# The second attention's normalisation moved by a step each, its transpose into another PSUM bank, and its value pads written in one copy

## The chip, the cores and the metric

The kernel runs on one core of one Trainium2 chip. The metric is the device time of one execution in microseconds (us). A core has five engines with a queue each: TensorE (PE in the profile; its weight loads are PEld), VectorE (DVE), ScalarE (ACT), GpSimd (POOL) and SyncE (SP), which only issues DMAs here. PSUM, where TensorE's results land, has eight banks, and GpSimd does not work on it in this kernel.

## The reference

Two layers of a gated cross-attention block over x of 16 x 128 x 256 (batches, tokens, channels), with a context of the same shape:

```python
x = x + tanh(g_xattn[0]) * L0_xattn(layernorm(x), ctx, ...)   # first attention, fp8-rounded inputs, 16 heads of 128
x = x + tanh(g_ffn[0])   * L0_ffn(layernorm(x), ...)          # silu feed-forward
x = x + tanh(g_xattn[1]) * L1_xattn(layernorm(x), ctx, ctx, mask, ...)
x = x + tanh(g_ffn[1])   * L1_ffn(layernorm(x), ...)          # top-1 mixture of 8 experts
```

The change lies in the third line, the second attention. Its core, for each of the 16 batches:

```python
q = (Q @ w_q.T).reshape(B, S, 8, 4, 8)        # 32 heads of 8: 8 groups of 4
k = (K @ w_k.T).reshape(B, S, 8, 8)           # one key and one value head for each group
v = (V @ w_v.T).reshape(B, S, 8, 8)
scores = einsum("bnghd,bmgd->bnghm", q, k) / sqrt(8)
scores = where(pad or not causal, -inf, scores)
attn = softmax(scores, axis=-1)
out = einsum("bnghm,bmgd->bnghd", attn, v).reshape(B, S, 256)
return out @ w_o.T + b_o
```

## The kernel before

The program is unrolled. Its stages follow one another with some overlap: first attention (lines 239 to 665), feed-forward (694 to 732), second attention (858 to 1156) with the routing of the tokens to experts (785 to 856) woven in, and the experts (1169 to 1213).

**The second attention** is a loop over steps n (line 1123). A step is 8 of a batch's 32 heads, 128 queries by 128 keys each, so a batch is four steps and a pair of steps is one half (c) of the output's 256 channels. At step n the loop writes down, in this order:

- scores(n) and top(n): TensorE adds the mask (L992, an identity matmul in bf16) and the scores (L999) in a PSUM tile of two banks, of which there are two; VectorE takes the negated maximum of each row (L1006). The keys come as kb, each group's keys masked to one head's rows.
- probs(n - 1): TensorE transposes the exponentials e of the step before (L1034, eight 128x128 blocks into two banks tagged tr), and VectorE copies them to eT (L1035, two copies).
- exp(n): ScalarE writes e, unnormalised (L1015, eight instructions), and GpSimd halves the rows three times by addition, to 16 partial sums for each row (L1021, L1022, L1023: half, half, part).
- values(n - 2), for odd n: VectorE sums the 16 partial sums of the pair's 16 heads (L1045) and takes the reciprocal (L1046); GpSimd spreads it over the 8 channels of a head (L1048: rr, one buffer); TensorE multiplies eT with the value pads (L1052, 16 matmuls, each to 32 output rows) into o, the first half of the PSUM bank tagged pv.
- divide(n - 3), for even n: TensorE transposes rr into the second half of the same bank (L1067), ScalarE copies that to rsum in SBUF (L1069), and VectorE multiplies o with rsum into oT (L1070).
- keys of the batch two steps ahead: GpSimd makes kb (L970, two instructions), TensorE the values (L976, PSUM tag mm), and VectorE copies them four times (L981) into the value pad. A pad holds, for each group and each of its four heads, 32 columns of which only the head's own 8 aren't zero, so that the four heads' matmuls add up to 32 output rows. There are two pads, zeroed once.
- for every fourth batch's start, the front of the next group of four: load, norm, transposes (L940), query and key projections (L952, tag mm).
- the routing's stages, then output of batch (n - 4) // 4 when its last step's division is done: TensorE projects oT (L1076, tag mm), VectorE adds the bias (L1078) and the residual (L1082) into a row. When a routing group (4, 4, 4, 3 and 1 batches) is complete, routing starts: norm, transposes, the router's matmuls (L798, tag mm), its decision on VectorE, prefix counts by matmul (L827, L828, tag mm), and then for each batch a store of the plain row (SP, L856) and a scatter of the row to its expert's slot (GpSimd's queue, L845). The experts' loads wait for all scatters.

PSUM's eight banks in this stage: four for the scores, two tr, one pv, one mm. So all users of mm follow one another, each waiting until the one before has been read out.

**What sets the order.** Semaphores and buffers are handled by a tile framework. It also orders each engine's instructions: a planner runs through the program with its own forecast of times and gives a free engine the ready instruction that ranks first, by the written order (the score matmuls rank 100 places earlier). So an engine's order can differ from the written one, and once set it is fixed: on the chip an engine waits at the head of its queue.

```python
    for n in range(-2, N1 + 5):
        ...
        if 0 <= n - 2 < N1:
            values(n - 2)
        if 0 <= n - 3 < N1:
            divide(n - 3)
```

Of the kernel before, what the change touches and what calls it, by code (L numbers as in the profile page):

```python
# [9 lines left out]
F32 = mybir.dt.float32  # L10
# [5 lines left out]
ALU = mybir.AluOpType  # L16
AX = mybir.AxisListType

P = 128
B = 16  # L20
DM = 256
KD = DM // P
# [13 lines left out]
def flamingo_kernel(  # L36
# [27 lines left out]
    nc = tc.nc  # L64
# [4 lines left out]
    NH, NG, HD = 32, 8, 8  # L69
# [4 lines left out]
    psum = psum0.enter_context(tc.tile_pool(name="psum", bufs=2, space=bass.MemoryType.PSUM))  # L74
# [36 lines left out]
    ident = const.tile([P, P], F32, name="ident")  # L111
# [127 lines left out]
    with (  # L239
# [74 lines left out]
        class Unit:  # L314
# [162 lines left out]
            def scores(self, c):  # L477
                qT = self.qT.pop(c)
                pscore = ps_sc([P, 4, P])
                for j in range(4):  # L480
                    nc.tensor.matmul(  # L481
                        pscore[:, j, :], qT[:, j, :], self.kT[:, 2 * c + j // 2, :],
                        start=True, stop=True,
                    )
                self.sc[c] = pscore

            def top(self, c):
                mx = small.tile([P, 4], F32, tag="mx", name="mx")
                nc.vector.tensor_reduce(mx, self.sc[c], AX.X, ALU.max, negate=True)  # L489
                self.mx = mx  # L490
# [12 lines left out]
            def recip(self, c):  # L503
                sums = self.e[c][1]
                nc.vector.reciprocal(sums, sums)  # L505

            def divide(self, c):
                e, sums = self.e[c]
                nc.gpsimd.tensor_tensor(  # L509
                    e, e, sums[:, :, None].to_broadcast([P, 4, P]), ALU.mult  # L510
                )
# [10 lines left out]
            def values(self, c):  # L522
                eT = self.eT.pop(c)
                pv = ps_pv([P, 4, P])
                for g in range(2):
                    gg = 2 * c + g
                    nc.tensor.matmul(  # L527
                        pv[:, 2 * g : 2 * g + 2, :], self.vt[:, gg * P : (gg + 1) * P],
                        eT[:, 2 * g : 2 * g + 2, :], start=True, stop=True,
                    )  # L530
                self.pv[c] = pv
# [212 lines left out]
    NQ = NH // NG  # L744
# [151 lines left out]
    vpads = [cq.tile([P, NG, NQ, 32], F32, name=f"vpad{i}") for i in range(2)]  # L896
# [61 lines left out]
        else:  # L958
            nc.scalar.copy(f[i][:, c, :], pm)

    kbs, vps, es, eTs, oTs, scs, mxs, sums, pvs = {}, {}, {}, {}, {}, {}, {}, {}, {}

    def keys(b):

        g, j = divmod(b, G)
        f = front[g]
        tok = slice(j * P, (j + 1) * P)
        kb = ap.tile([P, KD, NQ, P], F32, tag="kb", name="kb")
        for c in range(KD):
            nc.gpsimd.tensor_tensor(  # L970
                kb[:, c], f[1][:, c, None, tok].to_broadcast([P, NQ, P]),
                hmask[:, :, None].to_broadcast([P, NQ, P]), ALU.mult,
            )
        pm = psum.tile([P, NG, HD], F32, tag="mm", name="ps_mm")
        for k in range(KD):
            nc.tensor.matmul(  # L976
                pm, f["cT"][:, k, tok], av[:, k, :], start=(k == 0), stop=(k == KD - 1)
            )
        vp = vpads[b % 2]
        for i in range(NQ):  # L980
            nc.vector.tensor_copy(vp[:, :, i, HD * i : HD * i + HD], pm)  # L981
        kbs[b], vps[b] = kb, vp

    def scores(n):
# [53 lines left out]
    def values(n):  # L1038

        if n % 2 == 0:  # L1040
            return
        b, c = n // 4, n // 2 % 2
        r = small.tile([P, 16], F32, tag="sum16", name="sum16")
        part = sums.pop(n // 2)
        nc.vector.tensor_reduce(r, part.rearrange("p i h t -> p (i h) t"), AX.X, ALU.add)  # L1045
        nc.vector.reciprocal(r, r)  # L1046
        rr = ap.tile([P, 16, HD], F32, tag="rr16", name="rr16", bufs=1)
        nc.gpsimd.tensor_copy(rr, r[:, :, None].to_broadcast([P, 16, HD]))  # L1048
        o = psum.tile([P, 2, P], F32, tag="pv", name="ps_pv", bufs=1)
        for h in range(NQ):  # L1050
            for q in range(4):
                nc.tensor.matmul(  # L1052
                    o[32 * q : 32 * q + 32, 0, :], vps[b][:, 4 * c + q, h, :],
                    eTs[n - 1 + q // 2][:, q % 2, h, :],
                    start=(h == 0), stop=(h == NQ - 1),
                )
        pvs[n] = o, rr

    def divide(n):

        if n % 2 == 0:
            return
        b, c = n // 4, n // 2 % 2
        o, rr = pvs.pop(n)
        if c == 0:
            oTs[b] = ap.tile([P, KD, P], F32, tag="oT", name="oT")
        nc.tensor.transpose(o[:, 1, :], rr.rearrange("p h d -> p (h d)"), ident)  # L1067
        rT = ap.tile([P, P], F32, tag="rsum", name="rsum", bufs=1)
        nc.scalar.copy(rT, o[:, 1, :])  # L1069
        nc.vector.tensor_tensor(oTs[b][:, c, :], o[:, 0, :], rT, ALU.mult)  # L1070

    def output(b):
        oT = oTs.pop(b)
# [26 lines left out]
    for g in range(B // G):  # L1100
# [3 lines left out]
        for b in range(g * G, (g + 1) * G):  # L1104
# [8 lines left out]
    ap = f2.enter_context(tc.tile_pool(name="a1", bufs=2, side="right", reuse_waits="tile"))  # L1113
    psum = f2.enter_context(
        tc.tile_pool(
            name="psum1", bufs=1, space=bass.MemoryType.PSUM, reuse_waits="tile"
        )
    )


    N1 = 4 * B
    routes = []
    for n in range(-2, N1 + 5):
        if 0 <= n < N1:
            scores(n)
            top(n)
        if 0 <= n - 1 < N1:
            probs(n - 1)
        if 0 <= n < N1:
            exp(n)  # L1130
        if 0 <= n < G:
            down(B - G + n, hd, psum.tile([P, DM], F32, tag="mm", name="ps_mm"))
            if n == G - 1:
                tp.close()
                ep = ctx.enter_context(tc.tile_pool(name="e1", bufs=2, reuse_waits="tile"))
        if 0 <= n - 2 < N1:
            values(n - 2)
        if 0 <= n - 3 < N1:
            divide(n - 3)
        m = n + 2  # L1140
        if m % 4 == 0 and 0 <= m < N1:
            keys(m // 4)
        g, i = divmod(n + 12, 16)
        if 1 <= g < B // G:
            front_step(g, i)
        for stages in routes:
            next(stages, None)
        m = n - 4
        if m % 4 == 3 and 0 <= m < N1:
            output(m // 4)  # L1150
            for b0, count in ROUTES:
                if m // 4 == b0 + count - 1:
                    routes.append(route(b0, count))
    for stages in routes:
        for _ in stages:
# [4 lines left out]
    psum = ctx.enter_context(  # L1160
        tc.tile_pool(
            name="psum2", bufs=2, space=bass.MemoryType.PSUM, reuse_waits="tile"
        )
    )
# [4 lines left out]
    for e in range(NE):  # L1169
# [12 lines left out]
        for f in range(NFC):  # L1182
            ph = ps_mm([P, CAP])
            for k in range(KD):
                nc.tensor.matmul(
                    ph, w1t[:, k, f * P : (f + 1) * P], xT[:, k, :],
                    start=(k == 0), stop=(k == KD - 1),
# [3 lines left out]
        for c in range(NCC):  # L1191
            po = ps_sc([P, DM])
            for f in range(NFC):
                nc.tensor.matmul(
                    po, hT[:, f, c * P : (c + 1) * P], w2t[:, f, :],
                    start=(f == 0), stop=(f == NFC - 1),
# [8 lines left out]
                    ap=xe[:, c, 2 * DM + 1 : 2 * DM + 2].bitcast(I32), axis=0  # L1205
# [79 lines left out]
```

## Time and profile before

| | |
|---|---|
| median of 3 runs | 1578.25 us (1572.7 to 1580.31) |
| the profiled execution | 1577.98 us, span from first to last instruction 1576.2 us |
| mean granted TensorE clock over the span | 0.950 |
| busy over the span: PE, DVE, ACT, POOL | 88%, 67%, 52%, 53% |
| first attention, from its first projection to its last residual | 27.0 to 953.6 us |
| second attention, from its first score to its last division or output | 1083.7 to 1432.8 us |
| experts | 1441.2 to 1572.4 us |
| L1045, sum, 128x16 out of 128x256, on VectorE | 32 times, 413 ns |
| L1046, reciprocal, on VectorE | 32 times, 247 ns |
| L1048, rr, on GpSimd | 32 times, 300 ns |
| L1067, transpose of rr | 32 times, 307 ns |
| L1069, rsum, on ScalarE | 32 times, 281 ns |
| L1070, division, on VectorE | 32 times, 280 ns |
| L981, value pad, 128x64, on VectorE | 64 times, 213 ns |
| L1078, bias, 128x256 out of PSUM, on VectorE | 16 times, 411 ns |

The columns of a group in the profile are: line, engine, operation, output and inputs, shapes and count, busy time, mean duration of one, idle time of the engine in front of it and what ended that. "A <- B: us, times, longest" in a list of waits says that A's engine stood idle until B released it. In a list in order of time the first two numbers are start and duration (us from the span's start), merged over instructions that follow one another; the brackets give the idle time in front and who ended it. Matmuls of fp32 operands show as two records each. The granted clock is 1 or 0.5 at any time; a mean between them is a mixture.

### The profile page before, as it was taken

The numbers are of one execution on the slowest core, as the hardware profiler recorded it, in microseconds if no ns is written. First come the engines' busy times: TensorE is split into PE (matmuls) and PEld (weight loads), VectorE is DVE, ScalarE is ACT, GpSimd is POOL, SyncE is SP. The second block draws the span as 40 slices with busy tenths as digits, with TensorE's granted clock in tenths as the row PEclk, the third lists the DMA queues.
The fourth block names the chain that finished last, engine by engine and source line by source line (L and its number), as shares of the span: only waits on it lengthen the run. The fifth ranks groups of instructions, "written<-read, shape, count | busy, mean of one in ns | idle before, by whom it ended". The sixth has DMA issues, their size and how long they took to land. (4 is left out here: it accounts for less than half of the span.)

```text
span 1576.2 us, 23047 instructions
## 1 busy us (share of the span) xinstructions
PE 1390.5 (88%) x7620; PEld 1002.1 (64%) x7620; DVE 1050.9 (67%) x2821; ACT 819.5 (52%) x2452; POOL 835.7 (53%) x793
## 2 busy tenths in 40 slices
PE   2878798798988999999999978999898899885998
PEld 1567677676765777777777764555445455554887
DVE  8888878788798776767676753534667677773100
ACT  3666566566566666666666641534444455441121
POOL 4566666667677555565656552121766766661111
PEclk9999999999999999999999988999998979885999
DMA  4301001000022100000000007000300100001562
GB/s 122 107 6 31 14 11 35 11 18 14 11 80 65 48 25 11 21 11 21 11 17 14 8 24 210 8 0 1 114 24 8 48 4 35 8 35 61 176 195 78
DMA packets 51113, 68.59 MB, mean 44 GB/s; under 512 B 5292, under 2 KB 37740, under 8 KB 50993
## 3 DMA queue, kind: packets, MB, share of 16 engines
q1 hardware_dynamic: 36912, 41.31, 8.6%
q10 hardware_dynamic: 11456, 17.63, 3.4%
q0 software_dynamic: 2624, 8.16, 1.4%
q8 instruction: 61, 1.00, 0.3%
q14 instruction: 60, 0.48, 0.1%
HBM read 50.53 MB, written 16.81 MB: 43 GB/s over the span
## 5 line engine op out<-in xcount | busy, mean ns | idle before, releaser
L509 POOL TENSOR_TENSOR e<-e,sums 128x512 f32<-128x512 f32 x128 | 139.9, 1093 | 234.2 <-DVE sums L505 128.9
L497 ACT ACTIVATE e<-ps_sc,mx 128x128 f32<-128x128 f32 x512 | 181.4, 368 | 92.7 <-DVE mx L489 83.8
L454 POOL TENSOR_TENSOR raw<-raw,q_r 128x512 f32<-128x512 f32 x192 | 208.6, 1116 | 34.5 <-DVE q_r L180 33.3
L431 DVE BATCH_NORM_STATS2 q_st<-raw 128x6 f32<-128x128 f32 x768 | 173.9, 278 | 67.0 <-ACT raw L422 66.6
L1015 ACT ACTIVATE e<-ps_sc,mx 128x128 f32<-128x128 f32 x512 | 139.8, 385 | 90.0 <-DVE mx L1006 85.9
L565 PE MATMUL ps_acc<-wp,cat 128*128 128x512 f32 x512 | 161.4, 439 | 17.7 <-POOL cat L227 15.5
L227 POOL TENSOR_TENSOR cat<-e_t,e_e 128x1024 fp32r<-128x1024 bf16 x64 | 136.3, 2129 | 53.8 <-DVE e_t L221 52.2
L463 PE MATMUL ps_tr<-ident,raw 128*128 128x128 f32 x768 | 121.3, 286 | 46.7 <-POOL raw L454 44.3
L481 PE MATMUL ps_sc<-kT,qT 128*128 128x128 f32 x1024 | 141.0, 281 | 16.6 <-ACT qT L472 16.5
L481 PEld LDWEIGHTS ps_sc<-kT,qT 128*128 128x128 f32 x1024 | 131.9, 194 | 34.3 <-ACT qT L472 28.5
L463 PEld LDWEIGHTS ps_tr<-ident,raw 128*128 128x128 f32 x768 | 94.8, 146 | 84.5 <-POOL raw L454 59.3
L519 ACT COPY eT<-ps_tr 128x512 f32<-128x512 f32 x128 | 75.4, 589 | 139.4 <-PE ps_tr L517 139.2
L1021 POOL TENSOR_TENSOR half<-e 128x512 f32<-128x512 f32 x64 | 81.2, 1269 | 120.5 <-ACT e L1015 116.8
L527 PE MATMUL ps_pv<-eT,vt 128*128 128x256 f32 x512 | 133.4, 382 | 1.0 <-DVE cat_y L538 1.0
L565 PEld LDWEIGHTS ps_acc<-wp,cat 128*128 128x128 f32 x512 | 96.6, 195 | 57.7 <-POOL cat L227 22.5
L422 ACT COPY raw<-ps_mm 128x512 f32<-128x512 f32 x192 | 113.7, 593 | 28.4 <-PE ps_mm L410 26.1
L527 PEld LDWEIGHTS ps_pv<-eT,vt 128*128 128x128 f32 x512 | 97.1, 192 | 30.8 <-issue 8.6
L538 DVE TENSOR_TENSOR cat_y<-ps_pv,r_sm 128x512 bf16<-128x512 f32 x128 | 86.9, 679 | 39.6 <-PE ps_pv L527 39.4
L472 ACT ACTIVATE qT<-ps_tr,hv 128x512 f32<-128x512 f32 x128 | 101.0, 789 | 23.0 <-PE ps_tr L463 21.1
L489 DVE TENSOR_REDUCE mx<-ps_sc 128x4 f32<-128x512 f32 x128 | 87.2, 681 | 27.5 <-PE ps_sc L481 27.5
L497 ACT ACTIVATION_READ_ACCUMULATOR e<-ps_sc,mx 128x1 f32 x512 | 105.2, 205 | 0.0
L1034 PEld LDWEIGHTS ps_tr<-ident,e 128*128 128x128 f32 x512 | 62.1, 150 | 61.7 <-ACT e L1015 35.0
(232 smaller groups left out, 2944.4 us busy)
## 6 DMA issues: line engine op xcount, KB each, us to landing
w1t<-in_w ACTq DMA_DIRECT2D x8, 1024.0 KB, 5.1
w2t<-in_w ACTq DMA_DIRECT2D x8, 1024.0 KB, 5.6
disp<-empty SPq DMA_DIRECT2D x16, 257.0 KB, 8.3
xe<-disp SPq DMA_DIRECT2D x8, 514.0 KB, 3.7
stage<-in_wprojT SPq DMA_DIRECT2D x16, 256.0 KB, 2.8
xg<-in_x SPq DMA_DIRECT2D x4, 512.0 KB, 3.9
xb<-in_x SPq DMA_DIRECT2D x16, 128.0 KB, 2.0
ctx<-in_ctxT SPq DMA_DIRECT2D x16, 128.0 KB, 2.2
```

The costliest lines, as they stand in the source:

```text
L227: nc.gpsimd.tensor_tensor(dst, t[:, part], e[:, part], ALU.subtract)
L422: nc.scalar.copy(raw.rearrange("p h d -> p (h d)"), pm)
L431: nc.vector.bn_stats(self.st[:, 4 * blk + j, :], self.raws[blk][:, j, :])
L454: nc.gpsimd.tensor_tensor(src, src, self.r[:, 4 * blk : 4 * blk + 4, None].to_broadcast([P, 4, P]), ALU.mult,)
L463: nc.tensor.transpose(pt[:, j, :], src[:, j, :], ident)
L472: nc.scalar.activation(dst, pt, AF.Identity, scale=hv[:, col : col + 1], bias=hv[:, col + 1 : col + 2])
L481: nc.tensor.matmul(pscore[:, j, :], qT[:, j, :], self.kT[:, 2 * c + j // 2, :], start=True, stop=True,)
L497: nc.scalar.activation(e[:, j, :], pscore[:, j, :], AF.Exp, bias=self.mx[:, j : j + 1], accum_out=sums[:, j : j + 1],)
L509: nc.gpsimd.tensor_tensor(e, e, sums[:, :, None].to_broadcast([P, 4, P]), ALU.mult)
L527: nc.tensor.matmul(pv[:, 2 * g : 2 * g + 2, :], self.vt[:, gg * P : (gg + 1) * P], eT[:, 2 * g : 2 * g + 2, :], start=True, stop=True,)
L565: nc.tensor.matmul(self.acc, self.cat[c // 2][:, h % 8, :], wpr[self.cross, c][:, j, :, :], start=(h == 0), stop=(h == 15),)
L1015: nc.scalar.activation(e[:, i, :], s[:, i // NQ, i % NQ, :], AF.Exp, bias=mx[:, i : i + 1])
```

## The change

In values, the sum, the reciprocal and rr are taken out and become recip, which the loop writes at n - 3; rr has the pool's two buffers. values now has o to itself in the bank pv and copies it to oT at once, on VectorE. divide moves from n - 3 to n - 4, so to odd n; it transposes rr into a tile of the bank mm and multiplies oT in place by it, straight from PSUM, so ScalarE's copy and rsum are gone. output moves one step on, to n - 5, and the loop is one step longer. In keys, the four copies into the value pad become one, which reads each value four times and writes with a step of 40 elements from head to head (32 columns and 8).

```diff
-        vp = vpads[b % 2]
-        for i in range(NQ):
-            nc.vector.tensor_copy(vp[:, :, i, HD * i : HD * i + HD], pm)
+        vp = vpads[b % 2][:]
+        to = bass.AP(vp.tensor, vp.offset, [vp.ap[0], [P, NG], [32 + HD, NQ], [1, HD]])
+        nc.vector.tensor_copy(to, pm[:, :, None, :].to_broadcast([P, NG, NQ, HD]))
...
         b, c = n // 4, n // 2 % 2
+        o = psum.tile([P, P], F32, tag="pv", name="ps_pv", bufs=1)
+        for h in range(NQ):
+            for q in range(4):
+                nc.tensor.matmul(
+                    o[32 * q : 32 * q + 32, :], vps[b][:, 4 * c + q, h, :],
+                    eTs[n - 1 + q // 2][:, q % 2, h, :],
+                    start=(h == 0), stop=(h == NQ - 1),
+                )
+        if c == 0:
+            oTs[b] = ap.tile([P, KD, P], F32, tag="oT", name="oT")
+        nc.vector.tensor_copy(oTs[b][:, c, :], o)
+
+    def recip(n):
+
+        if n % 2 == 0:
+            return
         r = small.tile([P, 16], F32, tag="sum16", name="sum16")
         part = sums.pop(n // 2)
         nc.vector.tensor_reduce(r, part.rearrange("p i h t -> p (i h) t"), AX.X, ALU.add)
         nc.vector.reciprocal(r, r)
-        rr = ap.tile([P, 16, HD], F32, tag="rr16", name="rr16", bufs=1)
+        rr = ap.tile([P, 16, HD], F32, tag="rr16", name="rr16")
         nc.gpsimd.tensor_copy(rr, r[:, :, None].to_broadcast([P, 16, HD]))
-        o = psum.tile([P, 2, P], F32, tag="pv", name="ps_pv", bufs=1)
...
-        pvs[n] = o, rr
+        rrs[n] = rr
...
-        o, rr = pvs.pop(n)
-        if c == 0:
-            oTs[b] = ap.tile([P, KD, P], F32, tag="oT", name="oT")
-        nc.tensor.transpose(o[:, 1, :], rr.rearrange("p h d -> p (h d)"), ident)
-        rT = ap.tile([P, P], F32, tag="rsum", name="rsum", bufs=1)
-        nc.scalar.copy(rT, o[:, 1, :])
-        nc.vector.tensor_tensor(oTs[b][:, c, :], o[:, 0, :], rT, ALU.mult)
+        rT = psum.tile([P, P], F32, tag="mm", name="ps_mm")
+        nc.tensor.transpose(rT, rrs.pop(n).rearrange("p h d -> p (h d)"), ident)
+        nc.vector.tensor_tensor(oTs[b][:, c, :], oTs[b][:, c, :], rT, ALU.mult)
...
-    for n in range(-2, N1 + 5):
+    for n in range(-2, N1 + 6):
...
         if 0 <= n - 3 < N1:
-            divide(n - 3)
+            recip(n - 3)
+        if 0 <= n - 4 < N1:
+            divide(n - 4)
...
-        m = n - 4
+        m = n - 5
         if m % 4 == 3 and 0 <= m < N1:
             output(m // 4)
```

More of the change, by code (lines that the diff above doesn't have):

```diff
@@ L959, in qk @@
             nc.scalar.copy(f[i][:, c, :], pm)
-    kbs, vps, es, eTs, oTs, scs, mxs, sums, pvs = {}, {}, {}, {}, {}, {}, {}, {}, {}
+    kbs, vps, es, eTs, oTs, scs, mxs, sums, rrs = {}, {}, {}, {}, {}, {}, {}, {}, {}
     def keys(b):
@@ L1046, in values @@
         nc.vector.reciprocal(r, r)
-        rr = ap.tile([P, 16, HD], F32, tag="rr16", name="rr16", bufs=1)
+        rr = ap.tile([P, 16, HD], F32, tag="rr16", name="rr16")
         nc.gpsimd.tensor_copy(rr, r[:, :, None].to_broadcast([P, 16, HD]))
-        o = psum.tile([P, 2, P], F32, tag="pv", name="ps_pv", bufs=1)
[L1050 to L1056, printed above, removed]
-        pvs[n] = o, rr
+        rrs[n] = rr
     def divide(n):
```

## The prediction

> **What bounds the kernel now.** I read the page first, then the stretch of the second attention, its waits, and its instructions in order of time. The chain that ended last reaches back only to 1556.58 us, so it says nothing here. Slices 28 to 36 of the page (39.4 us each) are this stage:
>
> ```profile
> span 1576.2 us, 23047 instructions
> ...
> PE   2878798798988999999999978999898899885998
> ...
> PEclk9999999999999999999999988999998979885999
> ```
>
> TensorE is nine tenths busy in most of these slices, and the granted clock falls. The same stretch in one row:
>
> ```profile
> core 0: us, PE busy (x) PEld busy (x) DVE busy (x) ACT busy (x) POOL busy (x), PEclk, DMA share, GB/s
> 1085.00:1424.00 339.00, 300.02 (x2274) 174.14 (x2270) 242.55 (x548) 161.56 (x582) 218.78 (x274) 0.89 0.10 33
> ```
>
> TensorE is busy 300 of 339 us at a mean clock of 0.89. The clock record has only 1 and 0.5, so some 22% of the stretch, 75 us, ran at half clock; the work done there, 75 x 0.88 = 66 us, would take 33 us at full clock. No engine is full. Who waits, from 1110 to 1420 (total, times, longest, in us):
>
> ```profile
> ACT e L1015 <- DVE mx L1006: 75.4, 45, 6.0
> ...
> DVE sum L1045 <- POOL part L1023: 35.7, 13, 4.1
> ...
> PEld ps_tr L1034 <- ACT e L1015: 35.0, 28, 2.8
> ...
> PE ps_tr L1034 <- ACT e L1015: 12.8, 9, 2.0
> PE ps_pv L1067 <- POOL rr L1048: 12.2, 7, 3.5
> ...
> PE ps_pv L1052 <- DVE oT L1070: 4.2, 1, 4.2
> ```
>
> Three waits stop TensorE itself: 12.8 us for e, 12.2 us for rr, 4.2 us for oT. Behind the first is VectorE, which stood 35.7 us in its sum waiting for GpSimd's partial sums. The order of time shows how:
>
> ```profile
> 1165.13 1.13 PE L999 MATMUL ps_sc<-kb,qT 32*128 32x512 f32 x4
> ...
> 1168.74 0.29 POOL L1048 COPY rr<-sum 128x128 f32<-128x128 f32 x1
> ...
> 1169.09 0.33 PE L1067 MATMUL ps_pv<-ident,rr 128*128 128x128 f32 x1 [1.81 <-POOL rr L1048]
> ...
> 1169.80 0.45 POOL L1023 TENSOR_TENSOR part<-half 128x128 f32<-128x128 f32 x1
> 1170.28 0.42 DVE L1045 TENSOR_REDUCE sum<-part 128x16 f32<-128x256 f32 x1 [4.13 <-POOL part L1023]
> ...
> 1170.95 1.21 DVE L1006 TENSOR_REDUCE mx<-ps_sc 128x8 f32<-128x1024 f32 x1
> ...
> 1172.26 2.18 ACT L1015 ACTIVATE e<-ps_sc,mx 128x128 f32<-128x128 f32 x8 [2.48 <-DVE mx L1006]
> ...
> 1172.90 2.05 PE L1034 MATMUL ps_tr<-ident,e 128*128 128x128 f32 x8 [2.00 <-ACT e L1015]
> ```
>
> Step 16's scores (the 1.13 us row) end at 1166.26, but their maximum starts at 1170.95, 4.7 us later: VectorE stands in the sum of pair 14/15, whose last partial sum lands at 1170.25, because GpSimd was making the next batch's masked keys (L970, twice over 1 us). The order on an engine isn't the written one: that sum is written in step 17, and the planner put it before step 16's maximum. Meanwhile TensorE stands 1.8 us in front of L1067, since rr is queued on GpSimd behind the next step's first half sum, and then 2.0 us for e. After that the eight transposes take 2.05 us where they took 1.09 us at 1161.60: half clock. Scores of steps 16, 17, 18, 19, 20 start at 1165.13, 1169.78, 1177.72, 1181.13, 1185.72: 20.6 us a batch. TensorE's own need, from the gaps where nothing waits (1126.25-1123.62, 1157.53-1153.90, 1160.54-1157.53, 1165.13-1160.54), is 2.63 + 3.63 + 3.01 + 4.59 = 13.9 us without front and routing. In eight of the sixteen batches the first step's maximum starts over 5 us after the start of its scores, where 1.2 us is the least.
>
> [...] half-clock spells of 3.4 to 10.2 us follow the stalls. [...] o and the transposed rr share the bank pv, and L1052 waited 4.2 us for L1070. [...] the maximum sits behind the sum.
>
> **The change, part by part.** There are 32 pairs of steps and 16 batches.
>
> *Sum, reciprocal and rr one step on (recip).* The same 32 sums (413 ns), reciprocals (247 ns) and spreads (300 ns), with two rr buffers for one. On GpSimd the half sums queue behind rr, which waits 8.9 us for the reciprocal and 7.5 us for its single buffer; that second wait goes, and GpSimd, at 219 of 339 us, gains slack, not time. The sum now ranks behind one more step's maximum. I also count that output moves one step on, away from the step that has values: scores of step 16 then follow those of step 15 by about 3.7 us instead of 4.59 us (output's 0.76 us and a turn-round less), so the maximum is ready sooner against the partial sum. I take it that the planner then puts the maximum first. What is late next: the sum may still stand before step 15's eT copies or step 17's maximum. So I take half of the 12.8 us: -6.4 us. Bounds: 0 (order unchanged) to -12.8.
>
> *Transpose and division another step on (divide).* rr is then over a step old when TensorE reaches it; 12.2 us of waiting gone, whatever VectorE does, though it pays only if e is not what is late next. Bounds: 0 to -12.2; I take -12.2, as e is earlier by the part above.
>
> *Values copied at once.* pv is free after one copy; the 4.2 us wait goes: -4.2 (bounds 0 to -4.2). Removed: 32 ScalarE copies of 281 ns, 9.0 us on an engine busy 162 of 339 us: nothing on the path; without that cover 9.0 us. Added: 32 copies 128x128 from PSUM on VectorE. No row has one; the nearest, L1070 (same size, one PSUM input), is 280 ns, and starts 0.20 us before the next instruction. [...] Between 32 x 0.20 = 6.4 and 32 x 0.28 = 9.0 us I take 6.4. The division keeps its 280 ns, now with the transposed rr in PSUM instead of o.
>
> *Value pads.* Four copies of 64 elements (213 ns; 0.61 us for the four) become one of 256. The nearest row is L1078, 256 elements from PSUM, 411 ns[...]. 16 x (0.61 - 0.40) = -3.3 us of VectorE[...]; were the repeated reading slow, +0.4 us each would still be 6 us.
>
> VectorE's sum: +3.1 us on 242.6 busy of 339. TensorE's standing hides it; I count it in full, as little cover is left once the stalls go.
>
> *Another bank (mm).* mm is one bank with 58 users in the stage (16 keys, 16 outputs, 12 projections, 10 routing and 4 feed-forward tiles; 47 of them in the window of the waits); 32 transposes come in, each a hand-over before and after. What waits is TensorE, and behind it the next step's masks and scores. Today 13 waits on mm's VectorE readers (5.6 us for t, 4.3 us for the pads, weight load and matmul counted apart) come to about 5 us over 47 hand-overs, 0.11 us each: 64 x 0.11 = +7.0 us. Bounds: 0, to 64 x 0.75 = 48 us if every hand-over waits for an eT pair and the copy.
>
> *Moved with it.* Output goes one step on (sum t 0.41 us, row 0.76 us, 16 each), and with it the routing: 16 row stores on SP (0.33 us to issue; only the mask loads stand there) and 16 scatters on GpSimd (1.0 us each), passing one step's half sums. Same count, same queues; about nothing as long as later steps follow. At the end no step follows: there the chain from last sum to last output (1421.08 to 1429.72) loses the ScalarE copy, some 0.3 us, which I leave out.
>
> *Clock.* [...] Two thirds of the 33 us would be 22; I take -20. Bounds 0 to -33.
>
> Sum: -6.4 - 12.2 - 4.2 - 20 + 3.1 + 7.0 = -32.7 us on the profiled execution's own 1577.98 us (span 1576.2 and 1.8 around it), that is 1545 us. The median, 1578.25, stands 0.3 above it, so the same number serves. The stretch would take 306 us; TensorE at full clock needs 300 - 33 = 267 and VectorE 246, so neither forbids it.
>
> **Rivals.**
> *Order unchanged.* The planner places the sum when its own forecast has the partial sum ready and VectorE free; if that still falls before the next maximum, e is as late as now, TensorE only moves its waiting from rr to e, and the clock stays low. For: in the trace the sum ran ahead of a step written earlier. Against: output leaves that very gap. It gives -4.2 - 4 (a little clock) = 1570 us, half of it within 0.5%.
> *All stalls gone.* -29.2 - 33 + 3.1 + about 3 for hand-overs = 1522 us. Against: GpSimd is busy 219 of 339 us, in lumps, and still late.
> *mm decides (slower).* In place: the bank mm, at each transpose. Without the 7.0 us the gain is 39.7 us, and 64 hand-overs eat it up at 0.62 us each. At 0.75 us, 48 us: 1586 us. For: one bank, in-order VectorE whose eT pair alone takes 1.28 us. Against: 0.11 us today, and most users are a step apart.
>
> **How the numbers follow.** Forecast 0.58 (1545; own range 1527 to 1563), order unchanged 0.22 (1570), mm decides 0.12 (1586), all gone 0.08 (1522). The range, 1522 to 1577, leaves out mm decides and the slower edge of the unchanged order. About 0.5%, 7.9 us, is what a measurement of this kernel can tell from no change. Faster: 0.58 + 0.08 + half of 0.22 = 0.77; within: 0.10; slower: 0.13.
>
> **What would show it.** Right: TensorE's wait for rr near nothing; VectorE's wait for the partial sums under 15 us; first maximum of a batch within 3 us of its scores; clock over the stretch 0.95 or more; pads 16 x 0.4 us; no wait for oT at the values. Wrong: the sum still in front of a batch's first maximum with 4 us of idle, or waits of the transposes, keys and outputs on mm adding to tens of us.

## The result, and the profile after

The change takes 1573.86 us (median of 20 runs, 1569.9 to 1575.86) against 1577.28 us before in the same comparison: ratio 0.9977, interval 0.9969 to 0.9985, 3.6 us where 33 were forecast; inside the range, far from its number. The profiled execution's span went from 1576.2 to 1571.3 us. The page of the kernel after, with the same rows as before:

```profile
span 1571.3 us, 23024 instructions
...
PE   2888798898888999999999978999998888985998
...
PEclk9789999999999999999999998999998999886999
```

and the stretch of the second attention, in the columns of the row shown for before:

```profile
1085.00:1424.00 339.00, 300.71 (x2275) 170.29 (x2274) 249.55 (x533) 153.53 (x545) 216.68 (x274) 0.94 0.10 33
```

The clock came back, 0.89 to 0.94, yet TensorE is as busy as it was (300.0 then). Who waits, from 1110 to 1420; L1061 is now the sum, L1064 rr, L1046 the values, L1073 the transpose of rr, L1074 the division, L1082 the bias:

```profile
ACT e L1015 <- DVE mx L1006: 134.0, 51, 6.8
...
DVE sum L1061 <- POOL part L1023: 33.9, 22, 3.8
...
PE ps_tr L149 <- DVE eT L1035: 8.9, 3, 3.6
PE ps_mm L952 <- DVE oT L1074: 7.6, 5, 2.8
...
PE ps_tr L1034 <- ACT e L1015: 6.8, 8, 2.1
...
PE ps_mm L952 <- ACT kT L959: 3.1, 3, 1.6
...
PE ps_mm L1073 <- DVE t L1082: 2.6, 2, 1.3
...
PE ps_mm L952 <- DVE vpad L981: 2.2, 2, 1.2
...
PE ps_mm L1073 <- POOL rr L1064: 2.0, 1, 2.0
PE ps_mm L827 <- DVE oT L1074: 2.0, 1, 2.0
```

TensorE's wait for rr has gone from 12.2 to 2.0 us, that for e from 12.8 to 6.8, that of the values to nothing. In their place stand 17.5 us in front of users of mm (some 3 before) and 8.9 us in front of the routing's transposes (L149). VectorE still stands 33.9 us in its sum (35.7 before), now 22 times instead of 13. Two places in order of time show both:

```profile
1173.18 1.13 PE L999 MATMUL ps_sc<-kb,qT 32*128 32x512 f32 x4
...
1174.34 0.45 POOL L1023 TENSOR_TENSOR part<-half 128x128 f32<-128x128 f32 x1
...
1174.83 0.42 DVE L1061 TENSOR_REDUCE sum<-part 128x16 f32<-128x256 f32 x1 [0.74 <-POOL part L1023]
...
1175.71 1.23 DVE L1006 TENSOR_REDUCE mx<-ps_sc 128x8 f32<-128x1024 f32 x1 [0.18 <-issue]
...
1229.66 0.44 DVE L840 COPY row<-number 128x4 int32<-128x4 int32 x1 [4.20 <-DMA disp<-row,slot_s]
...
1231.80 0.27 DVE L1074 TENSOR_TENSOR oT<-oT,ps_mm 128x128 f32<-128x128 f32 x1
...
1232.13 1.98 PE L952 MATMUL ps_mm<-cT,ak 128*128 128x512 f32 x4 [2.82 <-DVE oT L1074]
```

Step 19's scores end at 1174.31, and their maximum starts 1.4 us later, because the sum of pair 16/17 is in front of it. At 1232 a key projection waits 2.8 us for mm, which a division holds; its transpose had been done since 1226.95 (L1073, 1226.62 for 0.33 us), but VectorE stood 4.2 us in a copy of the routing.

VectorE's order (mx = maximum of a step, eT = its two copies) says what became of the sums. Batch 4 starts with step 16, batches counted from 0:

```
before: mx15 eT14 sum12/13 sum14/15 | mx16 eT15 mx17 eT16 mx18 eT17 mx19 eT18 sum16/17 sum18/19 | mx20
after:  mx15 eT14 | mx16 eT15 sum14/15 mx17 eT16 mx18 eT17 sum16/17 mx19 eT18 | mx20 eT19 sum18/19
```

Here the sum at the end of a batch went back by one maximum and stands in front of the second instead of the first. That isn't so everywhere. Of the fifteen sums at the end of a batch that another batch follows, thirteen stood in front of the next batch's first maximum before, and seven still do in the change (batches 0, 2, 5, 6, 9, 10 and 13). The other sum of each batch moved forward: it stood behind the maximum of the batch's last step in nine of sixteen batches, and does so in three now. VectorE's idle time in front of the sums, added up by pairs over the stage: 35.9 us at the batch's end and 4.8 in its middle before; 22.0 and 15.3 after. Most of what one sum gave up, the other took. The first maximum of a batch now starts within 3 us of its scores' start in 13 of 16 batches, and over 5 us after it in one, eight before.

### The profile page after: what moved, and what is told of

It is laid out like the page before. It is cut to its first block, busy times and chain, and to the rows that moved or that the text cites. A ratio compares the mean times of both kernels' runs of the same rounds, so it can differ in the third digit from the quotient of the medians.

```text
span 1571.3 us, 23024 instructions
## 1 busy us (share of the span) xinstructions
PE 1388.7 (88%) x7620; PEld 996.2 (63%) x7620; DVE 1057.8 (67%) x2805; ACT 813.0 (52%) x2420; POOL 833.6 (53%) x793
## 5 line engine op out<-in xcount | busy, mean ns | idle before, releaser
L481 PE MATMUL ps_sc<-kT,qT 128*128 128x128 f32 x1024 | 140.1, 280 | 14.6 <-ACT qT L472 14.6
L422 ACT COPY raw<-ps_mm 128x512 f32<-128x512 f32 x192 | 113.8, 594 | 28.2 <-PE ps_mm L410 25.9
L527 PEld LDWEIGHTS ps_pv<-eT,vt 128*128 128x128 f32 x512 | 96.2, 190 | 30.8 <-issue 9.0
L472 ACT ACTIVATE qT<-ps_tr,hv 128x512 f32<-128x512 f32 x128 | 101.1, 789 | 21.6 <-PE ps_tr L463 19.7
```

Of the source, the lines that this page charges most:

```text
L422: nc.scalar.copy(raw.rearrange("p h d -> p (h d)"), pm)
L472: nc.scalar.activation(dst, pt, AF.Identity, scale=hv[:, col : col + 1], bias=hv[:, col + 1 : col + 2])
L481: nc.tensor.matmul(pscore[:, j, :], qT[:, j, :], self.kT[:, 2 * c + j // 2, :], start=True, stop=True,)
L527: nc.tensor.matmul(pv[:, 2 * g : 2 * g + 2, :], self.vt[:, gg * P : (gg + 1) * P], eT[:, 2 * g : 2 * g + 2, :], start=True, stop=True,)
```

## The experiments

All ratios are to the kernel before, run beside it; the columns from "stage" on come from the one profiled execution of each. "Stage" runs from the start of step 0's scores to the start of step 63's, so that each kernel does nearly the same work in it; TensorE's idle time is its length less its busy time.

| kernel | median us | ratio (interval) | stage us | TensorE busy, idle | clock | wait in sums (times) |
|---|---|---|---|---|---|---|
| before | 1577 to 1579 | | 328.7 | 292.7, 36.0 | 0.90 | 40.7 (15) |
| the change | 1573.86 | 0.9977 (0.9969-0.9985) | 326.5 | 292.8, 33.7 | 0.94 | 37.4 (22) |
| after_sum_later | 1558.55 | 0.9875 (0.9860-0.9890) | 313.9 | 288.4, 25.5 | 0.93 | 0 |
| before_sum_later | 1547.0 | 0.9812 (0.9799-0.9825) | 300.6 | 279.6, 21.0 | 0.95 | 0.6 (1) |
| after_T_in_pv | 1567.1 | 0.9934 (0.9920-0.9947) | 319.6 | 289.7, 29.9 | 0.93 | 37.9 (21) |
| after_Tpv_sum_later | 1543.54 | 0.9784 (0.9772-0.9797) | 294.9 | 278.1, 16.8 | 0.96 | 0 |
| pads_alone | 1581.81 | 1.0019 (1.0008-1.0030) | 333.8 | 297.9, 35.9 | 0.88 | 45.2 (18) |
| steps_alone | 1588.05 | 1.0053 (1.0037-1.0070) | 339.7 | 288.6, 51.1 | 0.90 | 64.2 (28) |
| bank_alone | 1596.59 | 1.0106 (1.0084-1.0128) | 348.2 | 300.0, 48.2 | 0.90 | 36.9 (18) |
| after_output_early | 1595.12 | 1.0099 (1.0084-1.0113) | 345.5 | 314.7, 30.8 | 0.86 | 35.0 (15) |
| before_sum_one_on | 1555.4 | 0.9862 (0.9839-0.9885) | 306.4 | 282.3, 24.1 | 0.94 | 3.8 (3) |
| before_keys_on_act | 1559.52 | 0.9888 (0.9871-0.9905) | 311.9 | 287.2, 24.7 | 0.93 | 31.5 (14) |
| steps_sum_later | 1551.66 | 0.9827 (0.9803-0.9850) | 306.3 | 279.8, 26.5 | 0.93 | 0 |
| pads_sum_later | 1554.69 | 0.9861 (0.9840-0.9882) | 307.6 | 281.7, 25.9 | 0.94 | 0.6 (1) |
| after_second_sum_later | 1570.27 | 0.9954 (0.9939-0.9970) | 321.4 | 291.6, 29.8 | 0.93 | 20.8 (12) |
| best_number_later | 1539.04 | 0.9766 (0.9748-0.9784) | 289.1 | 275.2, 14.0 | 0.97 | 0 |
| before_number_later | 1574.11 | 0.9983 (0.9972-0.9994) | 325.4 | 292.0, 33.4 | 0.90 | 49.8 (15) |

My theory after the result was that the waiting sums in front of maxima hold the stage, whatever else is moved; the rivals, that the new waits on mm ate the gain, and that TensorE's own waits for rr and pv are what counts.

### The sum held back, and the transpose out of mm

The sum keeps its data and its place in the program; an edge without a semaphore only tells the planner that it follows a later copy on the same engine.

```diff
-            nc.vector.tensor_copy(eT[:, i], pt)
+            eTi[n] = nc.vector.tensor_copy(eT[:, i], pt)
...
-        nc.vector.tensor_reduce(r, part.rearrange("p i h t -> p (i h) t"), AX.X, ALU.add)
+        ins = nc.vector.tensor_reduce(r, part.rearrange("p i h t -> p (i h) t"), AX.X, ALU.add)
+        if n + 1 in eTi:
+            tc.add_manual_dep(
+                ins.ins, eTi[n + 1].ins.name,
+                mybir.DependencyInfo(mybir.DependencyClass.NoSync, mybir.DependencyReason.DATA),
+                reason="the sum after the copies of step n + 1",
+            )
```

On the change:

> The kernel after, with each pair's sum held behind VectorE's second eT copy of the step after the pair (an ordering edge, no new wait on another engine). Theory A (the sum still waits for GpSimd at the head of VectorE's queue, only in front of another step's maximum): VectorE's wait for the partial sums falls from 39 us to under 10, and the kernel takes 1550 to 1562 us. Theory B (the gain was lost in the shared bank mm, at the steps with projections and routing): the wait falls as well, but the time stays within 4 us of 1574.

On the kernel before, with nothing of the change:

> The kernel before, with the same ordering edge and nothing else of the change. Theory A: the wait of 41 us for the partial sums goes and the kernel takes 1550 to 1565 us, about what the change itself was forecast to give. Theory B, and the view that rr reaching TensorE late is the stall: the transposes of rr wait all the more, since rr comes later and its transpose does not, so 1575 us or more.

The change with its transpose in pv's bank instead of mm, and that with the sums held back too:

```diff
-        rT = psum.tile([P, P], F32, tag="mm", name="ps_mm")
+        rT = psum.tile([P, P], F32, tag="pv", name="ps_pv", bufs=1)
```

> The kernel after, with the transposed rr in the bank pv again (a tile of its own, between one pair's values and the next) instead of mm. Theory B: TensorE's waits of projections for the division, 11.7 us with the weight loads, and those of the routing behind it go, 1560 to 1566 us. Theory A: within 4 us of 1574, as the sums stand where they stood.

> Both edits on the kernel after. If both theories hold and add up: 1540 to 1550 us. Theory A alone: as after_sum_later. Theory B alone: as after_T_in_pv.

One edge takes 31 us off the kernel before (29.7 by the ratio), nearly all of what the whole change was forecast to bring and more than its own expectation said. Waits of before_sum_later over its stage (its sum is L1047, rr L1056, the transpose of rr L1075):

```profile
PE ps_pv L1075 <- POOL rr L1056: 12.8, 11, 1.8
...
PE ps_tr L1036 <- ACT e L1015: 1.3, 2, 0.8
...
DVE sum L1047 <- POOL part L1023: 0.6, 1, 0.6
```

TensorE still waits 12.8 us for rr, as long as before, and the kernel is 31 us faster: what the moved division was to win need not be won. On the change, the edge gives 15.3 us and the other bank 6.8; together 30.3, so each is worth more with the other, the bank 15.0 us once the sums are held back (by the ratios 16.1, 6.8, 30.4 and 14.4). The bank's part lies where projections share mm: with the sums held back, batches 6 and 7 (steps 24 to 31) take 25.8 and 21.4 us with the transpose in mm and 21.5 and 17.9 without; batch 8, which has no projections, takes 14.1 and 14.0. after_T_in_pv lies just above its range, 1560 to 1566. So both accounts hold in part: the sums, and mm.

### The parts alone, and the output's move

pads_alone makes only the one copy into the pads. steps_alone moves the steps (reciprocal at n - 3, division at n - 4 but ahead of that step's values, output at n - 5), with o and the transposed rr in one bank, ScalarE's copy and four pad copies as before. bank_alone copies the values at once and uses mm, and has the pads in one copy too, with sum, division and output at the old steps. after_output_early is the change without its last move:

```diff
-        m = n - 5
+        m = n - 4
```

> The kernel before with the value pads in one copy and nothing else. By VectorE's time alone 3.3 us less work, most of it under other waits: 1575 to 1578 us. If the placing of the sums is what decides (Theory A), even this small edit can move it, since the planner fits sums into the gaps: in its order the sums of some first pairs of a batch now stand one maximum earlier, which costs where their partial sums are late: 1578 to 1584 us.

> The kernel before with the steps of the change and not its bank: sum, reciprocal and rr at n - 3, transpose, ScalarE's copy and division at n - 4 (written ahead of that step's values, so that o's bank is free for them), output at n - 5; o and the transposed rr share a tile of pv as before. Theory A: the sums leave the front of a batch's first maximum but stay ahead of an eT copy, so part of the gain: 1563 to 1570 us, near the 1567 us of the kernel after with its transpose in pv. If the steps give nothing without the early copy of the values, since o now stays in its bank for two steps and the next values wait for its division: 1576 us or more.

> The kernel after with its steps taken back (sum, reciprocal and rr with the values at n - 2 and one rr buffer, transpose and division at n - 3, output at n - 4), so values copied at once, transpose in mm, pads in one copy. Theory A and B together: the sums stand in front of a batch's first maximum again and mm is crowded, 1578 to 1588 us. The forecast's terms for the copy at once (4.2 us of waiting gone) and for mm (7 us) would give 1575 to 1582 us.

> The kernel after with output back at n - 4, so in the same step as the division that it needs. The forecast took output's move for what brings a batch's first maximum ahead of the sum: then the wait in front of the first maxima is back and the time 1577 us or more. If the sum's own later place in the written order does it, the first maxima stay ahead, and output waits for the division in the bank mm instead: 1574 to 1584 us, with TensorE waiting for the division before output's matmuls.

Each of these is slower than before; only the whole change comes out ahead, by 0.23%. The waits tell different stories. pads_alone does away with 48 instructions and changes the planner's order with them: the sums wait 45.2 us for 40.7. In steps_alone pv is held until the later division, and the next pair's values wait for it, 22.0 us from 1110 to 1420, beside 64.2 us in the sums. In bank_alone keys and routing wait for mm behind the division (8.5 and 7.3 us from 1110 to 1420), on top of 21.6 us for e in the stage; at 1596.6 us it lies above both of its ranges. In bank_alone all fifteen sums at a batch's end stand in front of the next first maximum; in after_output_early only four do, fewer than in the change: **it isn't the output's move that lets the first maximum go ahead.** Neither expectation's time came, 1595 us, and TensorE's wait for the division in front of output didn't show. Its loss lies mostly in two batches: 2 and 6 take 28.4 and 33.9 us (21.4 and 22.5 in the change), while batches 4 and 8 take 14.0. In batch 6 one sum, 24/25, stands 5.4 us in front of mx26, whose scores had been there for 5.8 us when it started.

### Is one place enough, and is it GpSimd's masked keys?

before_sum_one_on puts the edge one step earlier (n in place of n + 1): the sum at the batch's end then stands between the next batch's first and second maximum, as sum14/15 does in the change, but in all fifteen batches where the change has eight; the middle sums stand behind the maximum of their batch's last step in ten of sixteen batches (nine before).

> The kernel before, with an ordering edge that lets the sum of a pair follow VectorE's copies of the pair's second eT, one step earlier than in the kernel before with the sum held back (1547 us). The sum then stands behind the first maximum of the next batch and in front of the second one: the place that the change gives it. Theory (the change moved the sum by one place, and one place isn't enough because the partial sum is still not there): VectorE still waits 25 us or more for partial sums, and the time is 1565 to 1578 us. Rival (the place was right, and the change spent its gain on the bank mm and on its steps): 1555 us or less, and the sum waits under 15 us.

Two of the waits in its stage, lines as in before_sum_later:

```profile
PE ps_pv L1075 <- POOL rr L1056: 12.0, 7, 3.4
...
DVE sum L1047 <- POOL part L1023: 3.8, 3, 3.4
```

My expectation fell: held in that place in every batch, the sums leave 3.8 us of waiting, and the kernel is 21.6 us faster. The sums at the batch's end cost 22.0 us of waiting in the change. Some 12 us of that lie in the seven batches where the sum hasn't left the front of the first maximum, so the expectation's premise, that the change gives this place, was only half true. In the other eight the place is the same, and they wait 10.0 us there and 3.8 here. There the partial sum comes 4.2 us after its last exponential in the change and 5.4 here (means of eight), and VectorE reaches the sum 3.0 us after that exponential in the change and 5.6 here: VectorE comes earlier in the change; the partial sum isn't later. Scores of the batch's first and second step start 3.5 us apart in the change and 4.4 here, with output's matmuls in between; that is part of it, argued from these times, and the rest wasn't tried.

before_keys_on_act leaves VectorE's order as it was and lets ScalarE make the masked keys:

```diff
-            nc.gpsimd.tensor_tensor(
-                kb[:, c], f[1][:, c, None, tok].to_broadcast([P, NQ, P]),
-                hmask[:, :, None].to_broadcast([P, NQ, P]), ALU.mult,
-            )
+            for q in range(NQ):
+                nc.scalar.activation(
+                    kb[:, c, q], f[1][:, c, tok], AF.Copy, scale=hmask[:, q : q + 1]
+                )
```

> The kernel before, with the masked keys made by ScalarE (8 scaled copies of 128x128 a batch) in place of GpSimd's two products of 128x512. VectorE's order is that of the kernel before; no sum is moved. Theory (the stall is a sum standing in front of a maximum while GpSimd is busy with the masked keys): without that block the partial sums are there in time, VectorE waits under 15 us for them, and the time is near that of the kernel with the sum held back, 1545 to 1560 us. Rival (GpSimd is late by its half sums alone, 155 us of the stage): the wait for partial sums stays over 25 us and the time within 5 us of before, 1573 to 1583 us. Slower, about 1590 us, if the 8 copies (some 2.2 us a batch) delay ScalarE's exponentials.

The time came (17.4 us less), the mechanism didn't: the sums still wait 31.5 us. GpSimd's stage falls from 213.3 to 184.6 us busy, and what shrinks on TensorE is the wait for rr. The waits of its stage, lines as before:

```profile
DVE sum L1045 <- POOL part L1023: 31.5, 14, 5.0
...
PE ps_tr L1034 <- ACT e L1015: 11.6, 8, 1.9
...
PE ps_pv L1067 <- POOL rr L1048: 4.0, 5, 3.3
```

The wait for rr was 12.2 us before, and that of the values for the division, 4.2 us, doesn't appear. So the masked keys are a small part of why the sums wait (40.7 to 31.5 us): GpSimd's own three half sums, 2.7 us at least after the exponentials, are enough to make a sum in that place wait. The stage can be shortened by another way than the sums, then, which is why a wait's length is no price by itself. Through which waits all of the 17.4 us came isn't shown.

### Which of the two sums

after_second_sum_later has the edge on the change only where n % 4 == 1, so that every middle sum goes back behind its batch's last maximum and the other stays.

> The change, with only the second of the two sums of a batch (the pair of the batch's first two steps, which the change's order puts in front of the maximum of the batch's last step) held back behind VectorE's next two eT copies; the other sum stays where the change has it. Holding back both gave 1558.6 us, 15 us less than the change. Theory (the change moved one sum of a batch one place back and the other one place forward, and the second move took the gain of the first): most of the 15 us comes with this sum alone, 1559 to 1566 us, and the sums wait 12 times or fewer in the stage, not 22. Rival (what is lost is at the first sum, which still waits in front of the batch's second maximum): 1569 to 1576 us.

The wait in the middle sums is gone (20.8 us and 12 times are left), but the time falls by 3.6 us only: the theory that this move took the gain fell. The remaining 11.7 us to after_sum_later belong to the sum at the batch's end, which still stands in front of the first maximum in seven batches and of the second in eight.

### Steps and pads with the sums held back

> Only the moved steps of the change (reciprocal one step on, transpose and division another, output one on), o and the transposed rr in one bank with ScalarE's copy, four pad copies, and the sum held back. Compare with the kernel before with the sum held back, 1547 us. Theory (the later division holds the bank pv over two steps, so that the next pair's values wait for it whatever the sum does): TensorE's wait of the values for the division stays at 15 to 25 us, and the time is 1555 to 1565 us. Rival (that wait came from VectorE standing in the sum): it falls under 5 us and the time is 1543 to 1550 us.

> Only the value pads in one copy, and the sum held back. Compare with the kernel before with the sum held back, 1547 us. Theory (the pads alone lost 0.19% because they shifted the planner's order of the sums, not because of the copy): 1544 to 1548 us, as VectorE does 3.3 us less. Rival (one copy of 256 is ready later than the first of four, or reads PSUM slowly): 1550 us or more.

With the sums out of the way, the moved steps alone are neither better nor clearly worse than before_sum_later (the intervals overlap). TensorE's values still wait for the division that holds pv, 19.5 us in the stage, as expected; the time in between says that most of that wait is covered. The pads alone, by contrast, lose 7.7 us to before_sum_later, against what I expected, though the copy takes what was forecast (411 ns in place of four of 213). The trace of pads_sum_later, in batch 6:

```profile
1212.38 1.13 PE L999 MATMUL ps_sc<-kb,qT 32*128 32x512 f32 x4
...
1219.13 0.43 DVE L840 COPY row<-number 128x4 int32<-128x4 int32 x1 [5.65 <-DMA disp<-row,slot_s]
...
1219.48 1.21 DVE L1006 TENSOR_REDUCE mx<-ps_sc 128x8 f32<-128x1024 f32 x1
...
1221.95 3.78 PE L952 MATMUL ps_mm<-cT,ak 128*128 128x512 f32 x4 [4.54 <-ACT qT L957]
```

VectorE stands 5.65 us in a copy of four numbers into a routing row. In VectorE's order it is the first instruction to write that row, far ahead of its written place; it has no other input to wait for, and I take that for the planner's reason. On the chip it waits until the scatters of the routing that had the buffer last have read it. The maximum behind it starts 6.0 us after the end of its scores, and a projection waits 4.5 us in turn. It is the sum's stall once more, with another instruction. But before_sum_later has it too; over the stage, pads_sum_later first:

```profile
PE ps_mm L952 <- ACT qT L957: 9.3, 2, 4.8
DVE row L840 <- DMA disp<-row,slot_s: 8.6, 2, 5.6
...
DVE row L840 <- issue: 6.1, 1, 6.1
```

```profile
DVE row L840 <- DMA disp<-row,slot_s: 11.3, 3, 4.8
```

VectorE's wait there is 14.7 us with the one pad copy and 11.3 without. What is new is that TensorE's projections wait behind it, 9.3 us where before_sum_later has none, in batches 6 and 10, which take 29.8 and 28.6 us (25.0 and 21.4 there). So the order of instructions that the planner made is the likely cause of the 7.7 us, and not shown by an experiment: no run has the one pad copy with both the sums and this copy held back, and nothing else of the change.

### The second early waiter

```diff
-        nc.vector.tensor_tensor(slot, slot, loc, ALU.add)
+        added = nc.vector.tensor_tensor(slot, slot, loc, ALU.add)
...
-        nc.vector.tensor_copy(row[:, :, 2 * DM + 1].bitcast(I32), number[:, gsl])
+        num = nc.vector.tensor_copy(row[:, :, 2 * DM + 1].bitcast(I32), number[:, gsl])
+        tc.add_manual_dep(
+            num.ins, added.ins.name,
+            mybir.DependencyInfo(mybir.DependencyClass.NoSync, mybir.DependencyReason.DATA),
+            reason="the numbers after the slots",
+        )
```

On after_Tpv_sum_later, and on the kernel before:

> The change with the transpose in pv's bank and the sums held back (1543.5 us), and an ordering edge that lets the copy of the numbers into a routing row (4 elements, L840) follow the slots of its own routing, so that it can't take on the wait for the row's buffer (10.3 us of VectorE's idle time there) in front of a maximum. Theory (an early copy that waits is a stall of the same kind as the sum): that idle time is gone, 1534 to 1541 us. Rival (those waits are covered): 1541 to 1546 us.

> The kernel before with the same edge for the copy of the numbers alone, sums as they were. VectorE stands 10.7 us in front of that copy in the stage. Theory (a stall of the same kind): that idle time is gone and the time is 4 to 11 us less, 1566 to 1573 us. Rival (covered, or the sums take it over): within 4 us of before, 1573 to 1581 us.

The first is the fastest kernel of the study, 1539.04 us, 2.3% under before, and in the theory's range. By the ratios it gains 2.8 us on after_Tpv_sum_later, with intervals that overlap, so the gain isn't clear of noise; the profiled stage is 5.8 us shorter, and no idle time is left in front of that copy. On the kernel before, the idle time at that copy goes too, but the sums take it over (40.7 to 49.8 us) and 2.7 us of gain are left, 0.17%: the rival's case.

## Why the prediction was wrong

The stall that the prediction named was real: holding the sums back and nothing else brings most of what it forecast. The change doesn't hold them back. TensorE's idle time in the stage was to shrink by 12.7 us and shrank by 2.3; its busy time was to shrink by 20 and didn't. By the prediction's own steps:

- **Sum one step on, -6.4 us.** This is the step that failed: "I take it that the planner then puts the maximum first." Written order isn't the planner's: the maximum went first in eight of fifteen batches, where it had in two, and the batch's other sum moved forward in front of other maxima. VectorE's wait for the partial sums was to fall under 15 us and stayed at 33.9. TensorE's wait for e did halve, to 6.4 us in the stage, but part of it only changed its name (see the clock, below). Holding all sums back on the change brings 15.3 us, about half of what was missing.
- **Transpose of rr into another bank, +7.0 us.** Right in kind and, on the change as it is, in size: moving it out brings 6.8 us. But once the sums don't wait it costs 15.0, so the forecast's own situation had a dearer mm. The waits of mm's users behind the division, 7.6 + 2.0 us, the bank's other waits beside them, fell on the batches that have projections, where 0.11 us for each hand-over was an average over the quiet ones too.
- **Division, -12.2, and values, -4.2.** Both waits went, and their time did not. I added up TensorE's waits as if each were worth its length; the next thing that is late took over (L149 8.9 us, mm 17.5), and before_sum_later shows the reverse, a gain of 31 us with 12.8 us of waiting for rr left standing. Nor do the 4.2 us show what sharing a bank costs: o has one buffer, and L1052 waited to write the very o that L1070 still read. That the shared bank had a part in it isn't shown.
- **Clock, -20.** The clock did recover: 68.3 us of the stage were at half clock before and 37.5 after, and TensorE's busy time in them fell from 60 to 34 us, which is worth 13 us (transposes of e that follow one another start 109 ns apart at full clock and 214 at half, medians in the trace of before). But the work grew by as much: busy time at full clock and half of that at half clock add up to 262.6 us before and 275.8 in the change (266 to 267 in before_sum_later, after_Tpv_sum_later and best_number_later). About 6 of these 13 us are in e's transposes and 5 in the values. In the rows under this list, both groups of transposes in the change are at full clock; the second takes 1.91 us for 1.09, because it goes along with the eight exponentials that it reads. Such transposes, over 200 ns directly behind another one at full clock and with their exponential ended less than 0.35 us earlier, number 54 in the change, 14 before and 10 in best_number_later: a wait for e, piece by piece, that the profile counts as busy. The values are cut into 50 groups for 31, and the first matmul of a group at full clock adds some 227 ns where those behind it add 27 on average. (The query projections, 15.0 us for 11.9, fell in part into half-clock spells.)
- **When half clock comes.** That two thirds of the 33 us would come back was my estimate; no trace showed which stalls half clock follows. In before, the ten half-clock spells of the stage last 3.4, 6.8 or 10.2 us; in the 3.4 us in front of each, TensorE had stood 1.6 to 1.9 us in six, 2.1 to 3.4 us in three and not at all in one. With the stalls gone (best_number_later) the clock is 0.97 and TensorE's busy time 275.2 us. What exactly brings half clock on was not tried.
- **VectorE, +3.1.** The copy takes 283 ns, near the 280 of L1070, the row used, of which the forecast counted 0.20 us; the pads take 413, near the 411 of L1078, the row used, for which the 0.40 us counted was my estimate. VectorE's busy time over the stage rose by 7.2 us, twice the forecast. What that cost alone was not tried.
- **Output's move.** I took it for what brings the first maximum forward. after_output_early has that order without it. It is needed all the same: without it the change takes 1595 us.

The transposes of e over the stage, before and in the change, and two groups of them in the change:

```profile
L1034 PE MATMUL ps_tr<-ident,e 128*128 128x128 f32 x496 | 79.1, 303 | 12.8 <-ACT e L1015 12.8
```

```profile
L1034 PE MATMUL ps_tr<-ident,e 128*128 128x128 f32 x496 | 83.2, 297 | 6.4 <-ACT e L1015 6.4
```

```profile
1181.88 1.09 PE L1034 MATMUL ps_tr<-ident,e 128*128 128x128 f32 x8
...
1185.35 2.18 ACT L1015 ACTIVATE e<-ps_sc,mx 128x128 f32<-128x128 f32 x8 [3.42 <-DVE mx L1006]
...
1186.00 1.91 PE L1034 MATMUL ps_tr<-ident,e 128*128 128x128 f32 x8 [0.27 <-ACT e L1015]
```

The rival "order unchanged", 1570 us, is nearest in time and half right in kind: the order stayed in half of the batches and TensorE exchanged its waits, but it said that the clock stays low, which it didn't. "mm decides" was worth 15 us, not 48. With both failures taken away, sums and mm, the change takes 1543.5 us (after_Tpv_sum_later). That this is so near the forecast's 1545 is in part luck: TensorE's idle time falls by 19.2 us there, for 12.7, and its busy time by 14.6, for 20.

## What to carry to other kernels

VectorE took its queue in order here: in the change, step 19's maximum started 1.4 us after its scores were there, behind a sum that stood 0.74 us for its input. On such an engine, look for short instructions that wait for a slow producer in front of long-awaited ones, and pin them behind by an ordering edge before moving work by steps: here one such edge brought 1.9%, and the whole change 0.23%. Moving the text of a loop moves what a planner does with its neighbours too, so read the order it made, for every instance in the period. And a sum of an engine's waits is no forecast: ask of each what is late next.

## What the runs showed that I had not expected

- A 0.42 us reduction in the wrong place costs 31 us of 1577 (32 instances, 40.7 us of idle time), 28 of them in the stage, and nearly half of these through TensorE's clock: with the sums held back, TensorE is idle 15.0 us less and busy 13.1 us less for the same matmuls, at a clock of 0.95 for 0.90, and its busy time at half clock falls from 60 to 27 us. In the kernel before, 1.6 us of idle time within 3.4 us came ahead of five of the ten half-clock spells. The sums' stall is paid for twice here, as idle time and as slower matmuls after it.
- A higher clock isn't time by itself: 0.90 to 0.94 in the change, busy time unchanged, in part because a transpose that follows its exponential piece by piece counts as busy while it waits (1.91 us for a group of eight, 1.09 otherwise), in part because the values are cut into more groups (50 for 31).
- Four copies of 64 elements turned into one of 256 elements, 3 us less of VectorE, lost 0.19% alone and 7.7 us beside the held sums. The planner's order of other instructions changed with it in both, the likely cause.
